# Eight PSUM banks shared out anew among the products of a gate/up stage: three and five in place of two, two and four

## The chip, the cores and the metric

The kernel runs on one core of one Trainium2 chip. The time is that of the device in microseconds (us), from launch to end on the core; three runs were made of the kernel before. A profiled execution was made as well: its trace has a start and a length for each instruction on each engine. In the rows PE is TensorE's matmuls, PEld its weight loads, DVE is VectorE, ACT is ScalarE, POOL is GpSimd and SP is the engine whose queue issues most transfers. PSUM is the memory into which TensorE writes; per partition it has eight banks of 512 fp32 values, and the kernel gives each 128x512 product a bank of its own.

## The reference, cut to what matters

`x` has 2048 rows (tokens) of 1024 values. The result is the sum of `x`, a long convolution of the normalised rows, and a feed-forward block with weights of four bits.

```python
xn = _layernorm(x, axis=-1)
# the convolution: kernel K of length 1024 from the S4 parameters, through the FFT, plus D * xn
K = _s4_kernel(Lambda, p, q, B, Ct, step, L)
y = irfft(rfft(xn, n=2*L) * rfft(K, n=2*L), n=2*L)[..., :L] + D[0] * xn
# the feed-forward block: 2752 gate rows, 2752 up rows, group-wise scale and zero
g = xn @ dequantize(gate_Wq, gate_scale, gate_zero).T
u = xn @ dequantize(up_Wq, up_scale, up_zero).T
h = silu(g) * u
x = x + y + h @ dequantize(down_Wq, down_scale, down_zero).T
```

## The kernel before, in words

All matrices are held as two fp16 parts (high and low), and each product is taken in three passes (high x high, high x low, low x high). The gate/up products and the down product use a scheme of seven products for a 2x2 split of both operands, in place of eight.

The work goes in stages:

1. **Start** (to about 135 us): rows are loaded, normalised, split and transposed. The weight blocks j = 0 and 1 are multiplied in the plain way, by `gate_up_plain` (L659): a gate bank g and an up bank u for each of 8 units of 512 tokens, tags "B" and "D" of the PSUM pool.
2. **Gate/up units** (about 135 to 881 us): for the blocks j = 2 to 20 and the two token halves cp = 0 and 1, `gate_up(j, cp, ...)` (L597) does one unit, 38 in all. Each unit has seven products of 12 matmuls of 128x128x512, in four banks A, B, C and D:
   - product 1 into A; ACT copies A to B (L619); product 7 into C; ACT copies C to the tile hb (L625); product 6 onto B; ACT copies B to D (L629); product 2 onto A; ACT applies silu to A.
   - The remaining three products of a unit are run in the course of the next unit (`pending`, `rest`): `fifth` puts product 5 onto D, and DVE adds D into hb (L636); `fourth` puts product 4 onto C, ACT copies C to ha, DVE adds B into ha and multiplies by A; `third` puts product 3 onto D, ACT applies silu to D and DVE multiplies hb by D.
   - So the order on PE is product 1 of unit n, 5 of n-1, 7 of n, 4 of n-1, 6 of n, 2 of n, 3 of n-1. The last reader of A and of B is DVE in `fourth`, that of C is ACT in `fourth`, that of D is DVE in `third`.
3. **Beside the units**, on DVE, ACT and the queues: `load_w` unpacks, scales, combines, splits and transposes the gate/up weights of block j+1 (tiles raw, w, nat, wf); from j = 4 on `load_wd` does the like for the down weights (w<-SZT brings their scales; tiles wd, nd, WD) and `s4` computes the convolution kernel in small steps, with six products of its own (s4b, s4s0 to s4s3, s4y) in PSUM.
4. **Convolution and down product** (from 881 us on): other pools, eight banks of one tag.

The banks come from one pool `ps`. A call `bank(name, tag)` (L111) takes the next bank of its tag in turn, and its first writer waits until the last reader of the tile that had the bank is done. Tag "ps" has four banks, for A, C, the S4 products, the two `mix` products and the transposes of the start (`turned`, L207); tags "B" and "D" have two each.

The order of instructions on each engine is set when the kernel is built: a scheduler with a timeline of its own (L1405) places each instruction, and an engine then runs its instructions in that order. A change of the banks thus changes the order as well.

Of the kernel before, what the change touches and what calls it, by code (L numbers as in the profile page):

```python
# [25 lines left out]
F32 = mybir.dt.float32  # L26
# [4 lines left out]
PSUM = bass.MemoryType.PSUM  # L31
DRAM = bass.MemoryType.DRAM

P = 128
# [53 lines left out]
def build(nc, tc, x, xp, raw_d, sz_d, par_d, vct_d, tab_d, csrow_d, out):  # L88
# [3 lines left out]
    with es:  # L92
# [2 lines left out]
        cst = pool("cst", bufs=1)  # L95
        ea = ExitStack()
        pools = {"h": ea.enter_context(tc.tile_pool(name="h", bufs=4, reuse_waits="tile"))}
        psp = ea.enter_context(tc.tile_pool(name="ps", bufs=4, space=PSUM))

        XSP = [dr.tile([P, 2, 4, 512], F16, name=f"XSP{c}") for c in range(2)]  # L100
        HF = [dr.tile([7, P, NPAIR, 512], F32, name=f"HF{c}") for c in range(2)]
# [6 lines left out]
        def htile(name, tag="h"):  # L108
            return pools["h"].tile([P, 512], F32, tag=tag, name=name)

        def bank(name, tag="ps"):  # L111
            return psp.tile([P, 512], F32, tag=tag, name=name, **({} if tag == "ps" else {"bufs": 2}))

        V, A = Engine(tc, nc.vector), Engine(tc, nc.scalar)
        SP, G, PE = Engine(tc, nc.sync), nc.gpsimd, Engine(tc, nc.tensor)
# [32 lines left out]
        def xtile(cp, f):  # L148
            if (cp, f) not in xf:
                home, tag = (uxp, "ux") if f in (0, 1, 3) else (utp, "ut")  # L150
                xf[cp, f] = home.tile([P, 2, 4, 512], F16, tag=tag, name=f"x{cp}_{f}")
            return xf[cp, f]
# [54 lines left out]
        def turned(src, name):  # L207

            ps = bank(name).rearrange("p (a b) -> p a b", b=P)
            for b in range(4):  # L210
                PE.transpose(ps[:, b], src[:, P * b : P * b + P], ident)
            return ps
# [75 lines left out]
        with ea:  # L288
# [276 lines left out]
            def plain(ps, w, cp, c, ts=slice(0, 512), kq=None):  # L565


                xt = [xtile(cp, f) for f in ((3, 1), (7, 0))[c]]
                ks = [k for k in range(8) if kq in (None, k % 4 // 2)]
                for k in ks:  # L570
                    for n, (wi, xi) in enumerate(PASS):
                        PE.matmul(ps[:, ts], w(k, wi), xt[k // 4][:, xi, k % 4, ts],
                                  start=(k == 0 and n == 0), stop=(k == 7 and n == 2))

            def mix(cp, c):
                ps = bank(f"mix{cp}{c}")
                plain(ps, lambda k, wi: wtile(wi)[:, 16 + k, :], cp, c)
                return ps
# [18 lines left out]
            def gate_up(j, cp, wf):  # L597

                def prod(i, ps, start, stop):
                    fa, fb = PROD[i]  # L600
                    xt = xtile(cp, fb)
                    for kt in range(4):
                        for n, (wi, xi) in enumerate(PASS):
                            ends[0] = PE.matmul(
                                ps, wf[kt // 2][:, 14 * (kt % 2) + 2 * fa + wi, :], xt[:, xi, kt, :],
                                start=(start and kt == 0 and n == 0), stop=(stop and kt == 3 and n == 2),
                                skip_group_check=not start,
                            )

                def rest(i):  # L610
                    if len(pending) > i:
                        pending[i]()

                nm = f"{j}_{cp}"
                isc = 1.0 / (XS * WS)
                add, mult = ALU.add, ALU.mult
                bA, bB = bank("A" + nm), bank("B" + nm, "B")
                prod(1, bA, True, True)
                heads[j, cp] = A.copy(bB, bA)  # L619
                rest(0)  # L620
                bC = bank("C" + nm)
                prod(7, bC, True, True)
                tag = "h" if j % 2 else "e"
                hb = htile("hb_" + nm, tag)
                A.copy(hb, bC)  # L625
                rest(1)
                prod(6, bB, False, True)
                bD = bank("D" + nm, "D")
                A.copy(bD, bB)  # L629
                prod(2, bA, False, True)  # L630
                A.activation(bA, bA, AF.Silu, scale=isc)
                rest(2)

                def fifth():
                    prod(5, bD, False, True)
                    tails.append(V.tensor_tensor(hb, bD, hb, add))  # L636

                def fourth():
                    prod(4, bC, False, True)
                    ha = htile("ha_" + nm, tag)  # L640
                    A.copy(ha, bC)
                    V.tensor_tensor(ha, bB, ha, add)
                    V.scalar_tensor_tensor(ha, ha, HS * isc, bA, mult, mult)
                    pending[2] = lambda: third(ha)

                def third(ha):
                    prod(3, bD, False, True)
                    A.activation(bD, bD, AF.Silu, scale=isc)
                    V.scalar_tensor_tensor(hb, hb, HS * isc, bD, mult, mult)
                    finish_h(j, cp, ha, hb)  # L650

                pending[:] = [fifth, fourth, None]
# [6 lines left out]
            def gate_up_plain(j, cp, c, wf, by_tile=False):  # L659
                nm = f"{j}_{cp}{c}"  # L660
                isc = 1.0 / (XS * WS)
                bg, bu = bank("g" + nm, "B"), bank("u" + nm, "D")
                for ts in [slice(s * P, s * P + P) for s in range(4)] if by_tile else [slice(0, 512)]:
                    for kq in range(2) if by_tile else (None,):
                        for m, ps in ((0, bg), (1, bu)):
                            plain(ps, lambda k, wi: wf[k % 4 // 2][:, 8 * wi + 4 * m + k // 4 * 2 + k % 2, :],
                                  cp, c, ts, kq)
                h = htile("h_" + nm, "h" if j % 2 else "e")
                A.activation(h, bg, AF.Silu, scale=isc)
                V.scalar_tensor_tensor(h, bu, HS * isc, h, ALU.mult, ALU.mult)  # L670
                return h

            def finish_h(j, cp, ha, hb):
                nm = f"{j}_{cp}"
                if j == NJ - 1:
                    for c, h in enumerate((ha, hb)):
                        pc = wtemp("nat", [P, 2, 512], F16, f"hpl{nm}_{c}")
                        split(pc, h)
                        A.dma_start(HPL[cp][:, c, 0:2, :], pc)
                    return  # L680
                def emit(f, src):
                    SP.dma_start(HF[cp][f, :, j // 2, :], src)

                if j % 2 == 0:
                    emit(0, ha)
                    slots[cp] = (ha, hb)
                    return
                s0, s2 = slots.pop(cp)
                s1, s3 = ha, hb
                s4, s6 = (htile(f"s{n}_{nm}") for n in (4, 6))  # L690
                emit(1, s1)
                emit(3, s3)
                V.tensor_tensor(s4, s0, s2, ALU.subtract)
                emit(4, s4)
                V.tensor_tensor(s2, s2, s3, ALU.add)
                emit(2, s2)
                V.tensor_tensor(s0, s2, s0, ALU.subtract)
                emit(5, s0)
                V.tensor_tensor(s6, s1, s0, ALU.subtract)
                emit(6, s6)  # L700
# [254 lines left out]


            h0a = gate_up_plain(0, 0, 0, wt[0], by_tile=True)
            h1a = gate_up_plain(1, 0, 0, wt[1])
            finish_h(0, 0, h0a, gate_up_plain(0, 0, 1, wt[0], by_tile=True))
            finish_h(1, 0, h1a, gate_up_plain(1, 0, 1, wt[1]))  # L960
            for c in range(2):
# [29 lines left out]
            s4_steps = s4()  # L991

            gate_up(2, 0, wt[2])
            gate_up(3, 0, wt[3])
            for j in range(2, NJ):
                if 3 <= j < NJ - 1:
# [31 lines left out]
        bank = lambda name: psb.tile([P, 512], F32, tag="ps", name=name)  # L1028
# [150 lines left out]
        for cp in range(2):  # L1179
            home, tag = (gp, "g") if cp else (cvp, "cv")  # L1180
# [228 lines left out]
```

## Time and profile before

| | us |
|---|---|
| three runs | 1327.34, 1329.95, 1331.86 |
| median | 1329.95 |
| the profiled execution, whole | 1331.74 |
| its span, first to last instruction | 1330.0 |
| PE busy in it | 1274.0 |
| first matmul of the units | 134.8 |
| first matmul of the convolution | 878.2 |
| mean granted clock of TensorE | 0.990 |

The span is what the rows of the trace cover; the remaining 1.74 us of the execution lie around it. A row of a timeline has the start in us from the span's start, the length in us, the engine, the line, the operation, the tile written and the tiles read, the form, a count of merged instructions and, in brackets, the idle time of the engine before the row and what ended it. Nearly all rows have line L77, because a helper issues the instructions there; the tiles tell them apart. In names of tiles the numbers are left out: `A<-x,wf` is a matmul into a bank A, `D<-B` the copy of B to D, `ha<-B,ha` DVE's add of B into ha, `hb<-D,hb` the add of D into hb, `ha<-ha,A` and `hb<-hb,D` the last products.

A matmul of 128x512 takes about 380 ns in its row, but matmuls overlap: 24 that follow each other without a wait take 5.18 us from the first start to the next, 0.216 us each. "PE busy" therefore says little; idle time between matmuls is what tells.

### The profile page before, as it was taken

The numbers are of one execution on the slowest core, as the hardware profiler recorded it, in microseconds if no ns is written. First come the engines' busy times: TensorE is split into PE (matmuls) and PEld (weight loads), VectorE is DVE, ScalarE is ACT, GpSimd is POOL, SyncE is SP. The second block draws the span as 40 slices with busy tenths as digits, with TensorE's granted clock in tenths as the row PEclk, the third lists the DMA queues.
The fourth block names the chain that finished last, engine by engine and source line by source line (L and its number), as shares of the span: only waits on it lengthen the run. The fifth ranks groups of instructions, "written<-read, shape, count | busy, mean of one in ns | idle before, by whom it ended". The sixth has DMA issues, their size and how long they took to land. (4 is left out here: it accounts for less than half of the span.)

```text
span 1330.0 us, 20904 instructions
## 1 busy us (share of the span) xinstructions
PE 1274.0 (96%) x7880; PEld 751.9 (57%) x7880; DVE 987.9 (74%) x1344; ACT 669.2 (50%) x1208; POOL 182.8 (14%) x267
## 2 busy tenths in 40 slices
PE   5999899999999899989989998999999999999998
PEld 5644344444444344444444443456558888888887
DVE  6779967486886877786878777462738898779792
ACT  4867566656656474766568475420204433443330
POOL 3230001010100000000111000000000032256440
PEclk8999899999999999999999998999999999999999
DMA  6791958469887988888798887765837779799981
GB/s 225 173 218 31 196 152 186 97 163 251 212 229 159 240 217 207 223 210 232 191 264 224 216 215 180 216 213 187 333 122 292 273 202 265 238 262 274 285 181 48
DMA packets 358401, 276.04 MB, mean 208 GB/s; under 512 B 211668, under 2 KB 304668, under 8 KB 354204
## 3 DMA queue, kind: packets, MB, share of 16 engines
q1 hardware_dynamic: 335676, 261.59, 70.6%
q0 software_dynamic: 21760, 10.49, 6.6%
q10 hardware_dynamic: 864, 2.62, 0.5%
q8 instruction: 62, 1.02, 0.3%
q14 instruction: 39, 0.32, 0.1%
HBM read 132.36 MB, written 94.84 MB: 171 GB/s over the span
## 5 line engine op out<-in xcount | busy, mean ns | idle before, releaser
L77 PEld LDWEIGHTS <-wf 128*128 128x128 f16 x3960 | 375.7, 99 | 467.8 <-issue 45.2
L77 PEld LDWEIGHTS <-g 128*128 128x128 f16 x2940 | 287.6, 98 | 33.5 <-issue 0.2
L77 ACT ACTIVATE w<-w,sz 128x64 f32<-128x64 int32 x640 | 217.9, 427 | 74.9 <-DVE w L77 58.3
L77 PE MATMUL A<-x,wf 128*128 128x512 f16 x912 | 215.2, 385 | 13.4 <-ACT ha L77 5.3
L77 PE MATMUL D<-x,wf 128*128 128x512 f16 x912 | 211.5, 380 | 14.1 <-DVE hb L77 12.1
L77 PE MATMUL C<-x,wf 128*128 128x512 f16 x912 | 208.0, 381 | 2.8 <-DVE ha L77 2.6
L77 ACT CAST g<-a 128x2560 f16<-128x2560 f32 x42 | 97.5, 2324 | 182.1 <-PE cv L77 52.6
L77 PE MATMUL A<-b,g 128*128 128x256 f16 x1680 | 185.9, 273 | 0.0
L77 DVE TENSOR_TENSOR w<-w 128x256 f32<-128x256 f32 (+2 forms) x272 | 136.9, 527 | 61.2 <-ACT w L77 54.7
L77 DVE TENSOR_TENSOR g<-a,g 128x2560 f16<-128x2560 f32 x42 | 118.4, 2821 | 30.9 <-ACT g L77 30.9
L1261 POOL DMA_DIRECT2D out<-o x64 | 78.8, 2139 | 360.7 <-DVE o L77 348.2
L322 POOL TENSOR_SCALAR sz<-sz 128x16 f32<-128x16 f32 x42 | 18.6, 443 | 673.2 <-DMA sz<-in_sz 622.7
L77 PE MATMUL B<-x,wf 128*128 128x512 f16 x456 | 106.7, 384 | 1.8 <-ACT B L77 1.8
L77 ACT CAST nat<-w 128x896 f16<-128x896 f32 x76 | 68.3, 935 | 72.9 <-issue 34.4
L77 ACT CAST nd<-w 128x896 f16<-128x896 f32 x70 | 64.1, 933 | 68.9 <-DVE w L77 47.6
L77 DVE TENSOR_TENSOR nat<-w,nat 128x896 f16<-128x896 f32 x76 | 81.0, 1087 | 19.3 <-ACT nat L77 19.1
L77 PE MATMUL D<-b,g 128*128 128x256 f16 x840 | 94.0, 273 | 0.0
L77 DVE TENSOR_TENSOR nd<-w,nd 128x896 f16<-128x896 f32 x70 | 75.5, 1086 | 16.3 <-ACT nd L77 16.0
L77 PEld LDWEIGHTS <-x 128*128 128x128 f16 x576 | 52.4, 98 | 23.7 <-issue 2.7
L77 DVE SCALAR_TENSOR_TENSOR p<-cv,p 128x512 f32<-128x512 f32 x32 | 21.9, 688 | 50.3 <-PE cv L77 44.9
L77 PE MATMUL cv<-band,x 128*128 128x512 f16 (+3 forms) x384 | 57.1, 299 | 0.0
L77 PE MATMUL g<-x,wf 128*128 128x128 f16 (+1 forms) x336 | 48.8, 293 | 1.7 <-ACT wf L82 0.8
(145 smaller groups left out, 1203.8 us busy)
## 6 DMA issues: line engine op xcount, KB each, us to landing
a<-HF SPq DMA_DIRECT2D x28, 1280.0 KB, 8.1
WD<-nd SPq DMA_DIRECT2D x70, 448.0 KB, 4.4
b<-WD SPq DMA_DIRECT2D x49, 640.0 KB, 5.9
w<-SZT SPq DMA_DIRECT2D x80, 256.0 KB, 5.7
raw<-in_raw SPq DMA_DIRECT2D x65, 256.0 KB, 3.8
HF<-ha SPq DMA_DIRECT2D x54, 256.0 KB, 2.9
HF<-s SPq DMA_DIRECT2D x40, 256.0 KB, 3.0
HF<-hb SPq DMA_DIRECT2D x36, 256.0 KB, 3.6
```

Of the source, the lines that this page charges most:

```text
L77: return method(*args, **kw)
L322: G.tensor_scalar(sz[:, 0], sz[:, 0], WS, None, ALU.mult)
L1261: G.dma_start(dst, o[:, q], accum_op=ALU.add)
```

## The change

The tags "B" and "D" become one tag "BD" with three banks, and the tag "ps" gets five in place of four. Units take their banks in the order A (ps), B (BD), C (ps), D (BD); the plain units take g and u from "BD". The number of banks in use stays eight, and no operation is added or removed.

```diff
-        psp = ea.enter_context(tc.tile_pool(name="ps", bufs=4, space=PSUM))
+        psp = ea.enter_context(tc.tile_pool(name="ps", bufs=5, space=PSUM))
...
-            return psp.tile([P, 512], F32, tag=tag, name=name, **({} if tag == "ps" else {"bufs": 2}))
+            return psp.tile([P, 512], F32, tag=tag, name=name, **({} if tag == "ps" else {"bufs": 3}))
...
-                bA, bB = bank("A" + nm), bank("B" + nm, "B")
+                bA, bB = bank("A" + nm), bank("B" + nm, "BD")
...
-                bD = bank("D" + nm, "D")
+                bD = bank("D" + nm, "BD")
...
-                bg, bu = bank("g" + nm, "B"), bank("u" + nm, "D")
+                bg, bu = bank("g" + nm, "BD"), bank("u" + nm, "BD")
```

With it the banks pass on in this way (u12 is a unit, u11 the one before, u10 the one before that):

| first written in | bank before | bank after, no S4 product between |
|---|---|---|
| A of u12 | A of u10 | C of u9 |
| C of u12 | C of u10 | A of u10 |
| B of u12 | B of u10 | D of u10 |
| D of u12 | D of u10 | B of u11 |

An S4 product takes a turn of tag "ps". Before, the next A and C then stand one turn nearer to their forerunners (C of a unit can get the bank of A of the unit before); after, there is one bank more between them.

## Prediction

> **What bounds the kernel now.** I read the page first, then busy time by stretches, then the waits of TensorE (PE), then the timeline at its longest gaps. Names such as C10.1 (product bank C of weight block j = 10, token half 1) come from laying the program's order of instructions beside the trace, in which names have no numbers.
>
> The page's busy line, and three stretches (start:end, length, then busy time and count of PE, its weight loads, DVE, ACT and POOL, granted clock, DMA share, GB/s):
>
> ```profile
> PE 1274.0 (96%) x7880; PEld 751.9 (57%) x7880; DVE 987.9 (74%) x1344; ACT 669.2 (50%) x1208; POOL 182.8 (14%) x267
> ```
> ```profile
> 400.00:630.00 230.00, 212.69 (x1001) 96.57 (x1000) 179.49 (x318) 140.58 (x304) 16.02 (x36) 0.99 0.85 211
> 630.00:824.00 194.00, 183.38 (x836) 81.84 (x834) 147.73 (x241) 123.64 (x271) 18.05 (x30) 0.98 0.85 213
> ...
> 881.00:1330.00 449.00, 443.40 (x3756) 360.41 (x3753) 324.68 (x264) 128.16 (x75) 98.41 (x80) 1.00 0.78 231
> ```
>
> PE sets the end: from 881 on it is full. So a microsecond of PE idle saved or added in the gate/up units (135 to 881) moves the end by as much. A unit is 84 matmuls of 0.216 us, 18.1 us; there are 38. From 230 to 400 PE idles 1.3 us, from 400 to 824 27.9, and there, up to 630, VectorE (DVE) is 78% and ScalarE (ACT) 61% busy. The waits of PE between 230 and 880 (us in total, times, longest):
>
> ```profile
> PE D L77 <- DVE hb L77: 11.4, 3, 5.5
> PE A L77 <- ACT ha L77: 5.3, 3, 3.0
> PE A L77 <- DVE ha L77: 3.7, 3, 1.9
> PE C L77 <- DVE ha L77: 2.6, 3, 1.8
> PE s4s L77 <- ACT ha L77: 2.5, 2, 1.6
> PE D L77 <- ACT D L77: 2.0, 1, 2.0
> PE B L77 <- ACT B L77: 1.4, 2, 0.7
> ```
>
> Lines 2 to 5 are bank waits, 14.1 us: A, C or an S4 product wants the bank of a unit one or two before, whose last reader (ACT's copy of C to ha, or DVE's product with A) is late. The others, 14.8 us, are results that come late inside a unit. Banks of B and D end no wait of PE.
>
> **What the change removes.** With five banks A and C come back to a bank a full unit later. The ten that can be seen, by start-to-start gaps of matmuls, are S4 at 414 (1.1), A9.1 (0.5), C10.1 (2.0), A11.0 (1.5), C12.0 (0.4), C12.1 (0.65), S4 at 575 (1.7), A13.1 (2.0), A14.1 (3.2), A18.1 (1.2), 14.2 us in all, and a slow clock behind A14.1: its 12 matmuls took 4.44 us for 2.75, another 1.7. Gross: 15.9 us.
>
> **What it adds.** In the order B, D, B, D over three banks, D of a unit takes the bank of B of the unit before (last reader: DVE's add into ha), and B takes that of D two units before (last reader: DVE's product into hb). The first writer of either is an ACT copy, so the new wait stands on ACT; PE sees it only if the copy ends after PE comes to product 6 (B) or 5 (D). I took, for each of the 38 units, the end of that DVE reader less the start of the copy in this trace. It is positive 16 times for B (38.9 us) and 22 times for D (56.2 us). Two places, the copies of D10.0 and of D12.0 (window timeline: start, length, engine, what, count, idle before):
>
> ```profile
> 452.74 0.60 ACT L77 COPY D<-B 128x512 f32<-128x512 f32 x1
> ...
> 459.88 0.69 DVE L77 TENSOR_TENSOR ha<-B,ha 128x512 f32<-128x512 f32 x1
> ...
> 464.48 1.78 ACT L77 CAST nat<-w 128x896 f16<-128x896 f32 x2 [7.75 <-DVE w L77]
> ```
> ```profile
> 532.70 0.60 ACT L77 COPY D<-B 128x512 f32<-128x512 f32 x1
> ...
> 537.89 5.41 ACT L77 ACTIVATE w<-w,sz 128x64 f32<-128x64 int32 x16 [4.58 <-DVE w L77]
> ```
>
> At 452.74 ACT would now stand until 460.57 with the activations of A and D and the weight casts behind it. The rule of the Trainium skill that speaks against the change is in "TensorE: Matmul & The Clock Gate", specification table: the queues of ScalarE and VectorE are strict first-in first-out, so all that follows a waiting copy waits too. By the rule alone ACT loses 95 us. By the rows it loses little: after that copy it would have waited for DVE until 464.48 anyway (7.75), and after the one at 532.70 until 537.89 (4.58). What counts is the copy against PE's need: 461.15 against D10.0 at 458.54, 2.6 short. The reader of B for the second ends at 537.05: 537.65 against 536.62, 1.0 short. Over all units seven such shortfalls add up to 8.2 us (1.5, 0.2, 2.6, 0.2, 1.0, 0.5, 2.3).
>
> **What it moves.** The build reorders around the new waits. POOL's order is unchanged; on PE pieces of C that had been pulled forward go back; on ACT more weight work stands ahead of the copies, and DVE's order changes with it. Three moves count. (1) D3.1's copy goes behind eleven scalings of w (to 211.5; PE needs it at 208.0): 4.1 short, less seven C matmuls now ahead of it (1.5), and the 1.9 us of waits that follow at 212 to 217 go into it: +0.7. (2) D12.0's copy goes behind the 16 scalings of w27, 5.41 us. Their unpacking on DVE moves up about 3 us, so they end near 540.1: copy done 540.7, need 536.6, 4.1 short. (3) The late product 3 at 805.59 goes behind 3 matmuls of A19.1, and B19.0 and A19.0 (5.8 us), which covers the wait:
>
> ```profile
> 803.71 1.23 DVE L77 TENSOR_TENSOR w<-raw,w 128x1024 f32<-128x1024 int16 x1 [8.28 <-DMA w<-SZT]
> ...
> 805.59 1.86 PE L77 MATMUL D<-x,wf 128*128 128x512 f16 x4 [5.46 <-DVE hb L77]
> ...
> 807.25 4.68 PE L77 MATMUL B<-x,wf 128*128 128x512 f16 x12
> ```
>
> The gap there is 5.6 us, and the 16 matmuls behind it lose 2.7 more. The same page (Part 1) says that PE falls to half rate after an idle window of about 3.4 us; here 5.46 and 3.02 us of waiting slowed it and a gap of 3.6 at 690 did not, so I add it only where the row shows it. Likewise eight matmuls of A16.1 now fill 1.7 of the gap at 690. In the plain units u of block 1 (103.4) must now wait for the activation of g of block 0, which ended at 105.5: 2.1 us, covered because PE waits 4 us for weights at 134.8 to 141. Without that cover it costs 2.1.
>
> **The sum: what is late next.** The bank waits sit where ACT and DVE are behind. I went along PE with ACT and DVE at the times of this trace, shifted only by the moves above. (The new waits, which no row shows, lie between 0, if every copy keeps ahead of PE, and 14.0, the second rival; this walk is what I take.)
>
> - 414 to 427: the 1.6 us gained are spent waiting for B9.1's copy (426.49, behind a cast that waited 6.16 for a transpose). 0.
> - D10.0 starts 2.6 late, C10.1 no longer waits 2.0: +0.6. D10.1's copy is done at 481.15, PE began it at 481.40: -0.25. Less the 0.4 of C11.0 and of C12.0: -1.1.
> - D11.1's copy moves behind a cast that ends at 521.4: done at 522.0, needed at 518.1. With D12.0, +4.1. D12.1's copy (559.31) came late before too, so there only +1.3 is left.
> - S4 and A13.1: -1.7. A14.1: would be -6.6, but D14.0's copy waits for B13.1's bank (620.0): -3.0. B15.0's copy was late in both (646.33): -0.1.
> - 690 and A18.1 bring -1.3 by 794. At 805 PE gains 8.3 at most, then D19.0's copy (813.68, behind casts that wait for DVE's sums) and B19.1's (824.29, done 824.9; needed at 827.7) leave -2.9. Nothing later is short.
>
> Net about -3 us, +0.7 at the start being lost in the first of these waits. The profiled execution took 1331.74 (span 1330.0, 1.7 outside it), 1.8 above the median 1329.95. Less 3 it gives 1328.7, the median less 3 gives 1327.0: **1328**, own range 1323 to 1333.
>
> **Rivals.** *The banks were the cause (0.25).* If ACT and DVE move up with PE, 15.9 + 1.7 + 8.3 = 25.9 less the shortfalls 8.2 and half of the moved-order loss (4.1): about -14, 1317. For: where DVE's slack is, it follows PE (no PE wait at all from 703 to 770). Against: DVE is blocked by transfers (the scales w<-SZT, 8.28) that no bank frees. *The copies hold ACT (0.35).* One mechanism: ACT stands at a B or D copy until DVE has read the bank, the weight scalings behind it are late, DVE waits for those (it already waits 49.8 us for them from 230 to 880) and reads the next bank later still. It decides where shortfalls are not given back: D3.1 4.1, D10.0 2.6 and D12.0 7.3 with its scalings not moved up, 14.0, less 1.7 at 690, is +12: 1343. It starts to win once the summed lateness of D10.0 to D14.0 exceeds the 14.7 us freed there. *It does nothing:* excluded, since the banks and orders of the built program differ.
>
> **Chances.** A measurement of this kernel tells about 0.3%, 4 us, from no change. The likeliest case (0.40) lies mostly inside that, some of it faster: 0.12 / 0.25 / 0.03. The second gives 0.24 faster, 0.01 same; the third 0.33 slower, 0.02 same. Faster 0.36, same 0.28, slower 0.36. The range 1314 to 1343 takes in both rivals.
>
> **What would show it.** Right: no wait of A, C or s4s on a reader of ha; new waits of PE D and PE B on ACT's copies, near D10.0, D11.1, D12.0 and D14.0, of 8 to 15 us in all; the 5.5 us wait on hb gone and a wait for D's copy near 811. Wrong: PE idle from 400 to 630 below 8 us (first rival) or above 25 us, with ACT's copies waiting for DVE (second); or a stage after 881 that isn't 449 us long.

## The result, and the profile after

| | before | after |
|---|---|---|
| median, us (7 runs each, on one chip) | 1330.13 | 1334.58 |
| ratio, 95% interval | | 1.0028 (1.0015 to 1.0041) |
| again, with more runs (59 and 22) | 1331.99 | 1334.43 |
| ratio, 95% interval | | 1.0017 (1.0009 to 1.0025) |
| profiled execution; its span | 1331.74; 1330.0 | 1334.12; 1331.1 |

The kernel became slower by 2.4 to 4.5 us. That is a real loss, but by the ratios (0.17 and 0.28%) it is less than the 0.3% that the prediction took as the bound. The page's busy line and three stretches after:

```profile
PE 1275.5 (96%) x7880; PEld 752.1 (56%) x7880; DVE 989.4 (74%) x1344; ACT 671.0 (50%) x1208; POOL 183.6 (14%) x267
```
```profile
400.00:630.00 230.00, 216.41 (x1012) 97.76 (x1010) 181.73 (x319) 140.10 (x299) 19.80 (x36) 0.99 0.87 212
630.00:824.00 194.00, 182.13 (x830) 81.39 (x829) 145.72 (x239) 119.68 (x260) 15.70 (x30) 0.98 0.83 210
881.00:1331.00 450.00, 446.00 (x3773) 362.01 (x3770) 326.17 (x266) 129.40 (x78) 98.41 (x80) 1.00 0.78 231
```

From 400 to 630 PE idles 13.6 us (17.3 before), from 630 to 824 11.9 (10.6 before). The last stage, from the first matmul of the convolution to the end of the span, is no longer than it was (450.3 us, 451.7 before). So the loss lies before 881, and not in the stage that looked worst. The waits of PE from 230 to 880 after:

```profile
PE D L77 <- ACT D L77: 15.1, 9, 3.1
PE D L77 <- DVE hb L77: 7.1, 2, 6.1
PE B L77 <- ACT B L77: 5.8, 6, 1.6
PE A L77 <- ACT ha L77: 0.2, 1, 0.2
PE C L77 <- ACT ha L77: 0.2, 1, 0.2
```

The waits of A, C and the S4 products are gone (14.1 us, now 0.4). In their place PE waits 20.9 us for ACT's copies into B and D, before 3.4. To find where the end moved, I compared the start of each unit's first product (A) in the two profiles; positive is later after:

| at A of unit | time before | after less before |
|---|---|---|
| 5.1 | 263.9 | +1.6 |
| 9.0 | 395.1 | +2.4 |
| 15.0 | 638.3 | +0.3 |
| 16.0 | 676.1 | -0.3 |
| 17.0 | 715.9 | **+5.0** |
| 19.0 | 789.6 | +4.9 |
| 20.0 | 834.2 | +2.6 |
| first matmul of the convolution | 878.2 | +2.6 |

The 5.3 us lost between units 16.0 and 17.0 are one stall, before product 3 of unit 15.1, and the slow matmuls behind it. Timeline before (start, length, engine, what, and in brackets the idle time before it and what ended it):

```profile
676.08 2.75 PE L77 MATMUL A<-x,wf 128*128 128x512 f16 x12
...
678.21 3.27 SPq L77 DMA_DIRECT2D w<-SZT  x4
...
685.12 1.22 DVE L77 TENSOR_TENSOR w<-raw,w 128x1024 f32<-128x1024 int16 x1 [3.45 <-DMA w<-SZT]
...
689.27 0.68 DVE L77 TENSOR_TENSOR hb<-D,hb 128x512 f32<-128x512 f32 x1
...
690.01 2.32 PE L77 MATMUL D<-x,wf 128*128 128x512 f16 x10 [3.41 <-DVE hb L77]
...
692.16 2.75 PE L77 MATMUL B<-x,wf 128*128 128x512 f16 x12
```

and after:

```profile
675.76 2.75 PE L77 MATMUL A<-x,wf 128*128 128x512 f16 x12
...
680.37 3.58 SPq L77 DMA_DIRECT2D w<-SZT  x4
...
689.24 1.23 DVE L77 TENSOR_TENSOR w<-raw,w 128x1024 f32<-128x1024 int16 x1 [5.67 <-DMA w<-SZT]
...
693.39 0.68 DVE L77 TENSOR_TENSOR hb<-D,hb 128x512 f32<-128x512 f32 x1
...
694.13 1.01 PE L77 MATMUL D<-x,wf 128*128 128x512 f16 x2 [6.12 <-DVE hb L77]
694.93 4.97 PE L77 MATMUL B<-x,wf 128*128 128x512 f16 x12
```

PE waits for DVE's sum `hb<-D,hb`. What that sum reads has long been there, but it stands in DVE's queue behind `w<-raw,w`, which waits for the scales of the down weights, `w<-SZT`. The scales are asked for 2.1 us after A of unit 16.0 starts before the change (678.21 less 676.08), and 4.6 us after it with the change (680.37 less 675.76). In this profile they also land later (5.3 us from the end of their issue to DVE's start, 3.6 before). The stall grows from 3.4 to 6.1 us, and the matmuls behind it run at about half rate: the twelve of B take 4.97 us, not 2.75, and the clock granted from 694 to 700 is 0.55.

One correction to the description of the banks: the build gives a tile the bank that came free first, not the next in turn. Before the change most A take the bank of C two units back and most C that of A two units back; after it A takes that of A three units back and C that of C two units back. For B and D the table was right.

### The profile page after: what moved, and what is told of

It is laid out like the page before. It is cut to its first block, busy times and chain, and to the rows that moved or that the text cites. A ratio compares the mean times of both kernels' runs of the same rounds, so it can differ in the third digit from the quotient of the medians.

```text
span 1331.1 us, 20934 instructions
## 1 busy us (share of the span) xinstructions
PE 1275.5 (96%) x7880; PEld 752.1 (56%) x7880; DVE 989.4 (74%) x1344; ACT 671.0 (50%) x1208; POOL 183.6 (14%) x267
## 4 chain that ended last, share of the span: by engine, by line
PE 47%; DVE 13%; DMA 9%; ACT 7%; issue 5%; SPq 3%; ACTq 0%; DVEq 0%
PE A L77 18%; PE D L77 11%; PE cv L77 8%; DVE w L77 5%; ACT w L77 5%; PE C L77 4%; PE E L77 3%; DMA w<-SZT 3%; SPq L77 3%; PE B L77 2%; DMA wf<-nat 2%; DMA WD<-nd 2%; DVE ha L77 2%; DVE nd L77 2%; DVE hb L77 1%
## 5 line engine op out<-in xcount | busy, mean ns | idle before, releaser
L77 PE MATMUL D<-x,wf 128*128 128x512 f16 x912 | 215.2, 386 | 22.7 <-ACT D L77 15.6
L322 POOL TENSOR_SCALAR sz<-sz 128x16 f32<-128x16 f32 x42 | 22.5, 536 | 679.0 <-DMA sz<-in_sz 549.2
L77 DVE TENSOR_TENSOR w<-raw,w 128x1024 f32<-128x1024 int16 x20 | 24.4, 1220 | 34.7 <-DMA w<-SZT 33.1
```

Source lines behind the costliest of these rows:

```text
L77: return method(*args, **kw)
L322: G.tensor_scalar(sz[:, 0], sz[:, 0], WS, None, ALU.mult)
```

## The experiments

Ratios are to the kernel before, run on the same chip beside each, with 95% intervals. The chips differ from run to run, so two experiments are best compared by their ratios.

**Is it the number of banks?** (e1) One line of the changed kernel:

```diff
-        psp = ea.enter_context(tc.tile_pool(name="ps", bufs=5, space=PSUM))
+        psp = ea.enter_context(tc.tile_pool(name="ps", bufs=4, space=PSUM))
```

> The changed kernel with four banks in tag ps in place of five (one bank of the eight lies idle); B and D still share three. My theory: the fifth bank only lets A and C start earlier for weights and copies that come no earlier, so taking it away brings the waits of A, C and the S4 products back while the waits for late B and D copies shrink: the time stays near the changed kernel's 1334.6, between 1333 and 1339. Rival (the fifth bank gained the 14.2 us that its waits cost before, and the sharing of B and D took 18): 1346 to 1352.

Measured: 1333.11 us, 1.0011 (1.0003 to 1.0019). Waits of A, C and the S4 products come back (6.0 us from 230 to 880), those for B's and D's copies fall from 20.9 to 14.1 (18.2 with the one of D19.0, which this profile puts down to DVE's nat), and the time is no longer than with five. So in the changed kernel the fifth bank gains nothing. The stall at 690 isn't in this build, yet it is not level with the kernel before: PE waits 2.7 us for a copy of B at 733, with slow matmuls behind. So the stall at 690 is where the changed kernel loses, and not the only place where a build with these banks can.

Two other ways to share eight banks, written here as edits of the changed kernel: six for A, C, D, the S4 products and u with two for B and g (e3),

```diff
-        psp = ea.enter_context(tc.tile_pool(name="ps", bufs=5, space=PSUM))
+        psp = ea.enter_context(tc.tile_pool(name="ps", bufs=6, space=PSUM))
...
-            return psp.tile([P, 512], F32, tag=tag, name=name, **({} if tag == "ps" else {"bufs": 3}))
+            return psp.tile([P, 512], F32, tag=tag, name=name, **({} if tag == "ps" else {"bufs": 2}))
...
-                bD = bank("D" + nm, "BD")
+                bD = bank("D" + nm)
...
-                bg, bu = bank("g" + nm, "BD"), bank("u" + nm, "BD")
+                bg, bu = bank("g" + nm, "B"), bank("u" + nm)
```

and all eight under one tag (e4).

```diff
-        psp = ea.enter_context(tc.tile_pool(name="ps", bufs=5, space=PSUM))
+        psp = ea.enter_context(tc.tile_pool(name="ps", bufs=8, space=PSUM))
...
-            return psp.tile([P, 512], F32, tag=tag, name=name, **({} if tag == "ps" else {"bufs": 3}))
+            return psp.tile([P, 512], F32, tag="ps", name=name)
```

> Eight banks shared out in another way: two for B (and g), six for A, C, D, the S4 products and u. B no longer waits for a D, nor D for a B. My theory (new waits of B and D copies are what the change lost by, and bank waits of A and C are given back whatever is done about them): 1324 to 1331, most of the new waits gone and a few of the old ones with them. Rival (any spare bank lets PE run ahead into the same late weights and copies): within 2 us of before, 1328 to 1332, with stalls moved. If instead sharing of D is what hurts: 1333 or more.

> All eight banks under one tag, each tile taking the bank that came free first. My theory: the bank that came free first is one or more units old, so no copy stands at a bank that DVE still reads, and no matmul either: 1320 to 1330. Rival (the feed of weights by DVE, ACT and the queues sets the pace, with or without bank waits): 1328 to 1334, with the idle time of PE from 400 to 630 us still above 12 us, all of it before A (weights) and D and B (results late within a unit).

Measured: 1341.80 (1.0076, 1.0061 to 1.0091) and 1352.55 (1.0156, 1.0139 to 1.0173). Both theories and both rivals failed, for a reason that none of them had: the time goes in the start. (For six banks the third case, 1333 or more, fits by its number, but it put the loss on the sharing of D.) With one tag for the transposes there and for u, PE is busy 98.2 us of the first 135 with eight banks, 112.1 with six, 119.0 before; with eight, its transposes (tile wt) wait 15.7 us for ACT's copies out of their banks, with six 1.1, before not at all. From the first matmul of the units to the first of the convolution the kernel with eight banks neither gains nor loses: it is 24.2 us late at the one and 24.3 at the other. With six it is 12.9 late at the one and 9.0 at the other. So these two neither show nor refute that the feed sets the pace in the units, and they are no better share-out. (With six the kernel's result is wrong: D of units 11.1 and 13.1 then follows a narrow S4 product in its bank; see the last section.)

**Was the wait of u in the start covered?** (e7) The bank of one u, for which PE waits 1.9 us at 104.4, is taken from the other tag; no instruction changes its place on any engine.

```diff
-                bg, bu = bank("g" + nm, "BD"), bank("u" + nm, "BD")
+                bg, bu = bank("g" + nm, "BD"), bank("u" + nm, "ps" if (j, cp, c) == (1, 1, 0) else "BD")
```

> The changed kernel with one bank moved: the bank u of block 1, token half 1, first column half, which PE waits for at 104.4 us, comes from tag ps; the order of instructions stays as it is on every engine. The prediction's step (the 2.1 us are covered by the waits for weights at 134.8 to 141): the wait of PE's u goes, the waits of A for wf grow by about as much, and the time stays within 1 us of the changed kernel's. Rival (the cover isn't there, because the weights follow DVE and ACT, which PE's earlier products feed): 1.5 to 2.5 us below the changed kernel.

Measured: 1334.32, 1.0019 (1.0010 to 1.0028). The wait of u is gone, the waits of A for `wf` are 7.3 us (5.7 and 6.1 in the two profiles of the changed kernel), and the time is the same. Covered, as predicted. The same bank moved together with the order of the sum that is tried below (e8) gave 1330.33, 0.9989 (0.9980 to 0.9998), no faster than that order alone: covered there too.

**Did the copy of D15.1 delay the scales?** (e2) In the changed kernel this copy waits 1.92 us for DVE's reading of B15.0's bank, and the casts stand behind it. I took D of that unit alone from the other tag. (The kernel's result is then wrong, for this D follows a narrow S4 product in its bank; instructions and sizes are the same, and so is their order but for some 30 places on an engine.)

```diff
-                bD = bank("D" + nm, "BD")
+                bD = bank("D" + nm, "ps" if (j, cp) == (15, 1) else "BD")
```

> The changed kernel with one bank moved: D of unit 15_1 alone is taken from tag ps, so its copy no longer waits for DVE's read of B15_0. My theory (this one wait of ACT delays two casts, behind them the transfer of the down weights and the transfers of the scales on SP's queue, and so DVE's sum into hb): the stall of PE before the third product of D15_1 falls from 6.3 us to 3.6 or less, the slow matmuls behind it go, and the kernel comes to 1329 to 1332, 3 to 5 us below the changed one. Rival (the stall comes from the shifted order of DVE's work or from transfers that are late anyway): the stall stays above 5 us and the time within 1.5 us of the changed kernel's.

Measured: 1335.32, 1.0026 (1.0014 to 1.0037). My theory fell. Timeline of ACT, SP's queue and PE:

```profile
680.07 0.94 ACT L77 CAST nd<-w 128x896 f16<-128x896 f32 x1 [2.38 <-DVE w L77]
...
682.64 3.56 SPq L77 DMA_DIRECT2D w<-SZT  x4
...
694.67 4.26 PE L77 MATMUL D<-x,wf 128*128 128x512 f16 x10 [6.17 <-DVE hb L77]
```

The copy no longer waits, but the cast behind it now waits 2.38 us for DVE. The scales are asked for 4.7 us after A of unit 16.0, no sooner than with the wait. The copy's wait was hidden behind a delay that came down another way. (The stall's 6.17 us are not to be held against the 6.12: in this build the eight matmuls of A16.1 no longer stand in the gap. From unit 16.0 to 17.0 the kernel loses 4.7 us, with the wait 5.3 and 3.6 in two profiles.)

**Is the stall an accident of one execution?** (e9) The changed kernel again.

> The changed kernel as it is, beside the same runs of the kernel before, for a second profile of it. My reading of its first profile holds if the stall at 690 is again above 5 us with slow matmuls behind it, with the scales landing late ahead of the sum hb<-D,hb, and the ratio again 1.0015 to 1.004. If that stall is an accident of one execution, it is 3 to 4 us here and the loss stands elsewhere.

```profile
694.97 1.01 PE L77 MATMUL D<-x,wf 128*128 128x512 f16 x2 [5.01 <-DVE hb L77]
695.78 4.36 PE L77 MATMUL B<-x,wf 128*128 128x512 f16 x12
```

Measured: 1334.43, 1.0017 (1.0009 to 1.0025). The wait is 5.0 us and the 12 matmuls of B behind it take 4.36 us. The start of A moves from +1.6 us at unit 16.0 to +5.2 at 17.0. It is no accident.

**Take the sum from behind the scales.** In `load_wd` the scaling of the second half may not be placed ahead of the sum at hand, as that of the first half already is. This went into the kernel before (e5) and into the changed one (e6).

```diff
-                dequant(*mb)
+                with tc.issue_after(tails[-1].ins):
+                    dequant(*mb)
```

> The kernel before with one order changed: the second scaling of the down weights (DVE's w<-raw,w that waits for the scales w<-SZT) may not be placed ahead of the sum hb<-D,hb of the unit at hand. My theory (the stalls of PE at 690 and 805 exist because that sum stands in DVE's queue behind an instruction that waits up to 8.3 us for its scales): both stalls, 3.6 and 5.6 us, and the 2.7 us of slow clock behind the second go, some of it returns as later waits: 1321 to 1327, the waits of PE's D on DVE's hb falling from 11.4 us to below 4. Rival (the scales only then hold up the next weights, the feed sets the pace): within 2 us of before, the stalls moved to A or to copies.

> The changed kernel with the same order as in the run before it. My theory (of the changed kernel's loss the 5 us at 690 come from the sum hb<-D,hb standing behind the late scales, so both kernels differ no more once it doesn't): the stall at 690 goes and the time comes within 2.5 us of the kernel before with this order, on either side, and 5 to 10 us below the changed kernel. Rival (the waits of the B and D copies cost by themselves): it stays 4 to 8 us above the kernel before with this order.

Measured: 1330.25 (0.9995, 0.9986 to 1.0005) with the old banks and 1330.11 (0.9990, 0.9979 to 1.0000) with the new. DVE in the changed kernel with this order:

```profile
686.59 0.68 DVE L77 TENSOR_TENSOR hb<-D,hb 128x512 f32<-128x512 f32 x1
...
689.08 1.23 DVE L77 TENSOR_TENSOR w<-raw,w 128x1024 f32<-128x1024 int16 x1 [0.67 <-DMA w<-SZT]
```

The sum now comes first, the stall at 690 is gone, and the changed kernel is level with the old: its interval lies below that of the changed kernel as it was. So the loss of the change hung on that sum's place (the edit also moves some hundreds of other instructions, so this is a difference between two builds; e10 below moves one transfer alone). In the kernel before, my theory failed: 11.4 us of waits for hb go, and next to nothing is gained, because later waits take their place (C 9.9 us, D's copy 4.6, B's 4.8). The rival's time came true, but its cause, the feed, is not shown: 8.0 of the 9.9 us of C are bank waits.

```profile
PE C L77 <- DVE ha L77: 4.6, 2, 2.9
...
PE C L77 <- ACT ha L77: 3.4, 1, 3.4
```

**Why are the scales late?** (e10) Followed back from `w<-SZT`: they wait for a tile that DVE frees, DVE waits for weights that ACT scales, and ACT's cast `nd<-w` at 664 waits for the tiles nat, which the transposes `wf<-nat` free. SP's queue and ACT after the change:

```profile
657.00 0.58 ACT L77 COPY ha<-C 128x512 f32<-128x512 f32 x1
...
659.26 0.33 SPq L77 DMA_DIRECT2D HF<-ha  x1
660.03 8.04 SPq L77 DMA_TRANSPOSE wf<-nat  x4
...
664.23 1.78 ACT L77 CAST nd<-w 128x896 f16<-128x896 f32 x2 [2.10 <-DMA wf<-nat]
```

Before, the same transfer, the transposes and the cast, which did not wait:

```profile
654.22 0.33 SPq L77 DMA_DIRECT2D HF<-ha  x1
...
657.68 8.03 SPq L77 DMA_TRANSPOSE wf<-nat  x4
...
661.89 1.85 ACT L77 CAST nd<-w 128x896 f16<-128x896 f32 x2
```

After the change ACT's copy to ha stands behind 16 scalings (657.00, before 646.85), DVE's product with it ends at 659.24 (before 654.19), and the transfer of this product stands in SP's queue ahead of the four transposes. Why the build puts the copy there stays open. With the fifth bank PE does C of unit 15.0 ahead of product 4 of unit 14.1, which would suggest it; but with four banks (e1) PE does product 4 first, as before, and the copy is as late and the cast waits for the transposes just so:

```profile
657.68 0.56 ACT L77 COPY ha<-C 128x512 f32<-128x512 f32 x1
...
665.38 0.94 ACT L77 CAST nd<-w 128x896 f16<-128x896 f32 x1 [1.82 <-DMA wf<-nat]
```

The test moves that one transfer behind them; the order on PE, DVE and ACT stays.

```diff
-                    SP.dma_start(HF[cp][f, :, j // 2, :], src)
+                    with tc.issue_after(last[0].ins) if (j, cp, f) == (14, 1, 0) else nullcontext():
+                        SP.dma_start(HF[cp][f, :, j // 2, :], src)
```

> The changed kernel with one transfer moved on SP's queue and nothing else: HF<-ha of unit 14_1 stands behind the four transposes wf<-nat at 660 instead of ahead of them. My theory (that transfer waits for a product that the change made 5 us late; the transposes behind it free the nat buffers 2 us late, and the delay runs through ACT's cast nd<-w, the unpacking of the next weights, and the scales w<-SZT to the sum hb<-D,hb): ACT's cast no longer waits for wf<-nat at 664, the scales are asked for 2 us earlier against PE, the stall at 690 falls from 5.2 to 6.3 us to 2.5 to 4.5, and the time falls by 2 to 4.5 us below the changed kernel's 1334.4, to 1330 to 1332.4. Rival (the scales are late for another reason, as they were when the copy's wait was taken away): stall above 5 us, time 1333.5 to 1335.5.

```profile
656.69 9.08 SPq L77 DMA_TRANSPOSE wf<-nat  x4
...
661.80 1.78 ACT L77 CAST nd<-w 128x896 f16<-128x896 f32 x2
...
665.81 1.11 SPq L77 DMA_DIRECT2D HF<-ha  x1
...
691.47 1.01 PE L77 MATMUL D<-x,wf 128*128 128x512 f16 x2 [3.91 <-DVE hb L77]
```

Measured: 1332.42, 1.0007 (0.9993 to 1.0021), 2.0 us below the changed kernel. The cast doesn't wait, the scales are asked for 3.4 us after A of unit 16.0 (4.6 without, 2.1 before), and from unit 16.0 to 17.0 the kernel loses 2.0 us (5.3 and 3.6 in the two profiles without). What is left of the delay was not tested; the copy of D15.1, which again waits 1.92 us, stands on that way. The two intervals overlap, so by the times alone this would not be shown; the rows show it at its place.

**Both orders, and either banks.** Then all transfers `HF<-ha` of the even blocks from 4 on were kept behind the transposes, with and without the order of the sum, and once with four banks in place of five (the first edit above). The expectations stand in the order e11, e12, e13, e14, e15.

```diff
-                    SP.dma_start(HF[cp][f, :, j // 2, :], src)
+                    with tc.issue_after(last[0].ins) if f == 0 and j > 3 else nullcontext():
+                        SP.dma_start(HF[cp][f, :, j // 2, :], src)
```

> The changed kernel with the scaling of the down weights kept behind the sum hb<-D,hb, and every transfer HF<-ha of the even blocks from 4 on kept behind the transposes of the weights fetched with it. If a transfer ahead of the transposes costs at more than one place: 1325 to 1329, below the changed kernel with the scaling alone (1330.1) by 1 us or more. If the feed sets the pace whatever is moved: 1329 to 1331.

> The kernel before, with its two, two and four banks, and both orders of the run before this one: the scaling behind the sum hb<-D,hb, the transfers HF<-ha behind the transposes. If queue order is what set the pace and the share-out of banks hardly matters: within 4 us of the 1320.5 of the changed kernel with these orders, 1317 to 1324.5. If the banks begin to matter once the queues are out of the way: its bank waits of A, C and the S4 products (14.2 us in the kernel before) stay and it ends 5 to 12 us later, 1325.5 to 1332.5.

> The changed kernel with every transfer HF<-ha of the even blocks from 4 on behind the transposes, the scaling left as it was. If the two orders add up (5 us from the scaling, 10 from the transfers): 1323 to 1327. If the transfers help only where the sum no longer stands behind the scales: 1330 to 1334.

> The kernel before with that order of the transfers alone. If the transfers gain nothing with two, two and four banks, whatever the scaling: 1329.5 to 1333. If the kernel with both orders was only unlucky in how the build ordered the rest: 1320 to 1327.

> The changed kernel with both orders, but four banks in tag ps in place of five. If it is the fifth bank that gains the 9.6 us by which the changed banks beat the old ones under these orders: 1328 to 1332, with waits of A, C or the S4 products back. If the gain comes from sharing B and D, or from how the build ordered the rest: below 1325.

Measured, us and ratio to the kernel before:

| order | 2, 2 and 4 banks | 3 and 5 banks | 3 and 4 banks |
|---|---|---|---|
| as it was | 1331.99, 1 | 1334.43, 1.0017 | 1333.11, 1.0011 |
| sum ahead of the scaling | 1330.25, 0.9995 | 1330.11, 0.9990 | |
| transfers behind the transposes | 1330.41, 0.9985 | 1328.62, 0.9970 | |
| both | 1330.07, 0.9990 | **1320.52, 0.9910 (0.9895 to 0.9926)** | 1328.47, 0.9968 |

The one with both (four runs) is the fastest of all, 11 us below the kernel before and below both of its expectations; that with the transfers alone fell between its two. With both orders the share-out of banks is worth about 10 us (9.6 by the medians, 10.6 by the ratios), and the fifth bank about 8 of them (8.0 and 7.7). Waits of PE from 230 to 880 with both orders, old banks, the four of A and C:

```profile
PE A L77 <- ACT ha L77: 5.4, 3, 2.8
...
PE C L77 <- ACT ha L77: 3.8, 1, 3.8
PE A L77 <- DVE ha L77: 3.4, 3, 1.7
PE C L77 <- DVE ha L77: 3.1, 2, 1.6
```

and the new banks, the first four of all:

```profile
PE B L77 <- ACT B L77: 7.5, 7, 3.0
PE D L77 <- ACT D L77: 6.6, 6, 2.2
PE D L77 <- DVE nat L77: 4.5, 1, 4.5
PE A L77 <- ACT ha L77: 0.6, 1, 0.6
```

15.7 us of bank waits of A and C stand against 0.6. The waits for copies are 18.6 us with the new banks (the first three lines; the third is D19.0's, whose copy is late) and 9.6 with the old (B 4.9, D 4.7). So some 6 of these 10 us show in the waits. What stays open: each edit makes the build order hundreds of instructions anew, so these are differences between whole builds, and the 10 us were not followed place by place.

## Why the prediction was off

The prediction was 1328 us, 2 to 3 below the kernel before, with 1323 to 1333 as the range of its likeliest case; the kernel came out 2.4 to 4.5 us above, at 1334.4 to 1334.6 (inside the wide range that took in both rivals). By its own steps:

- **What it removes: right.** All ten waits that it listed went.
- **What it adds: right in kind, wrong in size.** PE's waits for copies of B and D rose from 3.4 to 20.9 us, not to 8 to 15. The four places named hold 6.8 us of them (D10.0 1.1, D11.1 0.3, D12.0 2.4, D14.0 3.1).
- **The start: right in sign.** D3.1 came late, and u's wait was covered (e7). +1.6 us in place of +0.7.
- **230 to 400, counted as nothing: 0.8 us off, by luck.** Two terms that the walk left out nearly cancel. The wait of A7.1 at 339 (1.3 us, a bank wait too) went with the slow matmuls behind it, -3.1 us; D7.1 waited 2.0 us for its copy and slowed the matmuls behind it, +3.9.
- **400 to 676: right at its end.** Predicted -0.1 at B15.0, measured +0.3 at 638 and -0.3 at 676. B15.0's copy comes late in both (646.33 and 646.85), so what was gained before it was given back there, as the likeliest case said. (On the way, the sum's -1.7 behind S4 and A13.1 would be -2.4 by its own waits; this wait wipes that out.)
- **690: the step that failed.** "Likewise eight matmuls of A16.1 now fill 1.7 of the gap at 690." They do stand there (686.12 to 688.0), but the end of the gap was taken from the old trace. DVE's sum `hb<-D,hb`, which ends it, moved: PE's wait for it was 6.1 us in place of 3.4, and from unit 16.0 to 17.0 the kernel lost 5.3 us. In the prediction's sum 690 and A18.1 together bring -1.2 us (from -0.1 to -1.3 by 794); measured, from 676 to 790, +5.2. These 6.4 us are more than the whole difference between -2.9 and +2.6 at the end of the units.
- **805: right.** The wait on hb went and a wait for D19.0's copy came, at 820 (3.15 us); -2.3 us where -1.6 was predicted.

The walk moved ACT's copies and took DVE's and SP's times from the trace before. The delay ran just there: a copy late in ACT's order made a product late, the product a transfer, and the transfer four others on SP's queue (e10 shows this last link by itself, 2.0 us; e6 that the loss goes when the sum stands ahead of the scaling). The second rival had this kind of mechanism, ACT's work late and DVE with it, but put it at D3.1, D10.0 and D12.0 and not through SP's queue. The first rival, that banks were the cause, failed in this kernel (taking the fifth away costs nothing, e1), yet it is the one that both orders bring near: there the banks do gain.

## What to carry to other kernels

When a change moves the order of work, walk every queue it passes, the transfers' queue among them: a store whose data come late holds up the loads behind it, and a result that is ready can stand behind an instruction that waits for a load. A wait that is removed is worth only what the next late thing leaves; if it is given back, look for what is late next and mend that, then try the change again: here it cost 2.4 us or more alone and was worth about 10 with two orders mended. To learn whether a wait costs, take away that wait alone and see if the next instruction starts sooner.

## What was not expected of the hardware

The length of an idle stretch alone did not tell whether the clock falls. Waits of 6.12 us, of 3.02 us (before, at 619) and of 2.01 us (after, at 364) were followed by matmuls at 0.43 us each for 3.4 to 5 us; waits of 3.41 us (before, at 690) and 3.15 us (after, at 820) were followed by full rate, 0.22. The granted clock tells more. In each trace it changes only at the borders of a fixed grid of cells of 3.41 us. Two cells of the profile after and two of that before (start:end, length, then busy time and count of each engine, granted clock, DMA share, GB/s):

```profile
361.48:364.89 3.41, 1.40 (x7) 0.58 (x6) 3.37 (x8) 3.41 (x6) 0.00 (x0) 1.00 1.10 259
364.89:368.31 3.42, 3.42 (x10) 1.22 (x8) 3.36 (x5) 1.12 (x2) 0.00 (x0) 0.50 0.93 283
```
```profile
684.85:688.27 3.42, 1.75 (x9) 0.69 (x7) 3.15 (x5) 2.28 (x7) 0.00 (x0) 1.00 1.00 328
688.27:691.68 3.41, 1.67 (x8) 0.78 (x8) 3.41 (x7) 1.07 (x2) 0.00 (x0) 1.00 0.81 199
```

The wait of 2.01 us lies in one cell, PE idles 59% of it, and the next cell gets half the clock. The wait of 3.41 us is cut by a border into 49% and 51% of two cells, and the clock stays. So it is in all 17 traces between 130 and 885 us. The clock fell behind 84 cells of full clock: PE had idled 59% or more of each (once 55%). It stayed full behind 3560 others: PE had idled 60% or less of each. (The narrow S4 products are left out of PE's work here; with them counted, some falls stand at 30 to 40%.) The Trainium skill ("TensorE: Matmul & The Clock Gate", Part 1) speaks of a free-running window of about 3.4 us and of half rate after at least one idle window. The window agrees with these traces; that all of it must be idle does not: about six tenths were enough.

The scales took 3.6 us from the end of their issue to DVE's start before (681.48 to 685.12), 5.3 and 3.2 in the two profiles of the changed kernel; why was not traced.

The two kernels in which a D that ACT fills comes behind a narrow S4 product in its bank (e2, e3) gave wrong results; those in which B and D come behind products as wide as themselves did not. The Trainium skill ("PSUM — Partial Sum Buffer", "The four PSUM rules") says that a product is added only to columns that TensorE wrote since the last first product cleared its marks, and replaces the rest, whatever another engine copied there; no run here tests this by itself.
